# A Strassen step over pairs of FFN tiles in an RWKV layer: the products on block 11 of two tiles done as seven of 256 columns

## The chip, the cores and the metric

The kernel runs on one core of a Trainium2 chip. Its time is the device time of one execution in microseconds (us). The median of three runs of the kernel before is 3050.48 us (3047.41 to 3051.21). One further execution was taken with the hardware profiler, and all views of the trace below are of that one. The core's engines are TensorE (PE; its weight loads are listed as PEld), VectorE (DVE), ScalarE (ACT), GpSimd (POOL) and SyncE (SP, which here only issues DMAs). Each engine works through its instructions in order.

## The reference

A layer of 4 batches of 2048 tokens with 512 channels, all in float32: layer norm, then an RWKV attention and a feed-forward part (FFN) side by side, both added to the input.

```python
xn = _layernorm(x)
x = x + attn(xn) + ffn(xn)

def attn(x):
    r, k, v = (einsum('btc,hc->bth', mu * x + (1 - mu) * shifted, W) for ...)
    wkv = wkv_v4(k, v, w, u)        # a scan over the tokens
    return einsum('bth,ch->btc', sigmoid(r) * wkv, Wo)

def ffn(x):
    up_gate = einsum('bsd,hd->bsh', x, W1)   # 512 -> 2048
    up_lin = einsum('bsd,hd->bsh', x, W3)
    hidden = fwht(silu(up_gate) * up_lin)
    return einsum('bsh,dh->bsd', hidden, W2) # 2048 -> 512
```

## The kernel before, in words

The tokens are done in eight blocks of 1024 (`TB`), each in two halves of 512 (`H`). Channels lie on the 128 partitions. Blocks 0 and 1 also make and store combined weights; blocks 2 to 7 (the third and later ones) are alike. A block does, in this order:

- tile 0 of the gate and linear part, then six pairs of projections for k, v and r (`projected_pair`, line 410),
- tiles 1 to 15 of the gate and linear part (`up`, line 440): tile j gives 128 channels of `silu(gate) * linear` for both halves of the block, in the buffer `unit(j)` with its halves h0 and h1,
- the down part (`down`, line 727), which multiplies by W2 (with the Hadamard transform folded in) and Wo, in 46 pieces.

A gate and linear tile is one 2 x 2 block product, its left side the gate and linear weights of the tile, its right side the two halves of the tokens. It is done in Strassen-Winograd form: seven products in place of eight (`seven`, line 352), each over `KH` = 2 blocks of 128 channels and 512 columns, that is two matmuls. A matmul in float32 shows as two MATMUL rows in the trace, so a product is four rows. The weights of a tile come as one chunk of seven forms (896 KB) into a ring of three chunks (`ring_a`); `group` (line 971) asks for the chunk two ahead.

The seven products go into five PSUM banks, named pa, pf, pb, pc and pd. `bank()` (line 115) hands the eight banks out in turn. In the order of the code a tile does:

1. pa: form 0 on m11 (this is the product "on 11"); ACT copies pa to pb
2. pf: form 4; ACT copies pf to s5, in SBUF
3. pb: form 5; ACT copies pb to pc; then the **tail** of the tile before: ACT does the tanh of its pc into h1, DVE does one step on h0 with pd and two on h1 with pc and pb
4. pa: form 1; ACT does the tanh of pa into h0
5. pb: form 3; ACT copies pb to pd; DVE does `h0 = (h0 + 1) * pa`, then `step()`, then `pb += s5`
6. pc: form 6; DVE does `pc += s5`, then `step()`
7. pd: form 2

The recurrence of the attention runs on DVE (with exponentials on ACT) between these steps. `wkv(h)` (line 268) is a generator of nine pieces for each of the four heads of 128 channels; `step()` (line 968) issues the next one. The projections' hooks take nine pieces, the first head; the 15 tiles offer 30 places for the other 27. Since every engine works in order, the place of a `step()` in the code is its place on DVE's queue.

In the down part six of the seven forms are split once more ("deep", line 687), into matmuls of 256 columns, whose weights come in pieces into eight slots (`pieces_w`, `piece`, line 563). The first seven pieces are asked for at tile 15 (line 1053).

Of the kernel before, what the change touches and what calls it, by code (L numbers as in the profile page):

```python
# [2 lines left out]

# [6 lines left out]
F32 = mybir.dt.float32  # L10
# [5 lines left out]
P = 128  # L16
H = 512
# [23 lines left out]
def tile_rwkv_attn_hadamard_ffn(  # L41
# [36 lines left out]

    down_w = dram.tile([2, 7, KH, P, QR, P], F32, name="down_w")
    deep_w = dram.tile([6, 7, P, QR, P], F32, name="deep_w")  # L80
    stat_d = dram.tile([n_blocks, 2, TB], F32, name="stat_d")


# [6 lines left out]
    sa, sb = (const.tile([P, OFF + TB], F32, name=n) for n in ("sa", "sb"))  # L90
    e1b, e1 = (const.tile([P, TB], F32, name=n) for n in ("e1b", "e1"))
    banks = [ps.tile([P, H], F32, name=f"bank{b}") for b in range(8)]
    turn = [0]

    NP = NF // 2

    def unit(j):
        return right[:, j // NP, j % NP, :]
# [14 lines left out]
        return flat[:, 0:size].rearrange(f"p ({' '.join(names)}) -> p {' '.join(names)}", **dict(zip(names, shape)))  # L113

    def bank():
        turn[0] += 1
        return banks[(turn[0] - 1) % 8]


    k_flat, v_flat = (t.rearrange("p b t -> p (b t)") for t in (k_sb, v_sb))  # L120
    tf_flat = tf.rearrange("p f k t -> p (f k t)")
    x_first, x_tok = (flat.rearrange("p (t c) -> p t c", c=C) for flat in (k_flat, tf_flat))
    spread = v_sb[:, 0:2, :]
    stage = [v_sb[:, 2 + s // 2, ts(s % 2, H)] for s in range(4)]
    u2_of = [e1b[:, ts(g, H)] for g in range(KH)]
# [257 lines left out]
    def seven_forms(t, a11, a12, a22, a21):  # L383

        sub = ALU.subtract
        pool.tensor_tensor(t[1], a21, a22, ALU.add)
        pool.tensor_tensor(t[2], t[1], a11, sub)
        pool.tensor_tensor(t[3], a12, t[2], sub)
        pool.tensor_tensor(t[0], a11, a21, sub)
# [1 line left out]
    def forms_in(t):  # L391
        seven_forms([t[:, n] for n in range(3, 7)], *(t[:, n] for n in range(4)))

    def load_parts(i, n):
        t = ring_a.tile([P, 7, KH, P], F32, tag="a", name=f"part_{i}_{n}")
        if is_first(i, n):
            sp.dma_start(out=t[:, 0:4], in_=wpart[n])
            forms_in(t)
        else:
            sp.dma_start(out=t, in_=part_w[n])  # L400
        return t

    def is_first(i, n):
        return i == (1 if n < 3 * KH else 0)
# [35 lines left out]
    def up(i, j, w, tail, step):  # L440

        keep_parts(i, 3 * KH + j, w)
        h0, h1 = unit(j)[:, 0:H], unit(j)[:, H:TB]

        def on11(pa):
            act.activation(h0, pa, AF.Tanh, scale=0.5)

        def on22(pa, pb, s5):
            dve.scalar_tensor_tensor(h0, h0, 1.0, pa, ALU.add, ALU.mult)
            step()  # L450
            dve.tensor_tensor(pb, pb, s5, ALU.add)

        def on12(pc, s5):
            dve.tensor_tensor(pc, pc, s5, ALU.add)
            step()

        pb, pc, pd = seven(f"{i}_{j}", w, right_of["up"], tail, on11, on22, on12)
        return (
            lambda: act.activation(h1, pc, AF.Tanh, scale=0.5),
            lambda: dve.tensor_tensor(h0, h0, pd, ALU.mult),  # L460
            lambda: dve.scalar_tensor_tensor(h1, h1, 1.0, pc, ALU.add, ALU.mult),
            lambda: dve.tensor_tensor(h1, h1, pb, ALU.mult),
        )

# [93 lines left out]
        program += deep(m, *which)  # L560
    DEEP_AT = (0, 4, 5, 6, 1, 3, 2)

    def piece(i, u):

        return pieces_w[:, (u + 4 - len(program if i else whole_program)) % 8]

    def load_piece(i, u):
        pieces = program if i else whole_program
        if u < len(pieces):
            kind, form, n = pieces[u]  # L570
            src = down_w[n[0], form, n[1]] if kind == "plain" else deep_w[form, DEEP_AT[n]]
            sp.dma_start(out=piece(i, u), in_=src)

    whole, lo, hi = slice(0, H), slice(0, H // 2), slice(H // 2, H)
    x11, x12, x22 = stage[0:2], stage[2:4], x22_of
# [9 lines left out]
    def difference(out, x0, x1):  # L585
        dve.tensor_tensor(out, x0, x1, ALU.subtract)
# [8 lines left out]
    class Down:  # L595
# [21 lines left out]
            self.matmuls(pt, self.u - 1, rows, cols, start)  # L617

        def matmuls(self, pt, u, rows, cols, start=False):
            w = piece(self.i, u)  # L620
            for n in range(QR):
                pe.matmul(
                    pt[:, cols], lhsT=w[:, n, :], rhs=rows[:, n, :], start=start and n == 0, stop=n == QR - 1,
                    skip_group_check=True,
                )
# [299 lines left out]
    diag_1 = first_diagonals(1, first_statistics(1))  # L925

    def order_of(i):
        rkv, (first, *rest) = range(3 * KH), range(3 * KH, 3 * KH + NF)
        return [first, *rest] if i == 0 else [first, *rkv, *rest]

    class Chores:

# [26 lines left out]
    for i in range(n_blocks):  # L959
        last = i + 1 == n_blocks  # L960
        if i % per_batch == 0:
            dve.memset(carry[:, :, 0:1], PP0)
            dve.memset(carry[:, :, 1:3], 0.0)


        pieces = (None for h in range(NB) for _ in wkv(h))

        def step():
            next(pieces, None)

        def group(n):

            order = order_of(i)
            if n + 2 < len(order):
                parts.append(load_parts(i, order[n + 2]))
            return parts.pop(0)


        tail = ()
        if i == 0:  # L980
            for kind, after in ((1, 2), (2, 0), (0, None)):
                w = w_next
                if after is not None:
                    w_next = load_square(i, after)
                    if kind != 1:
                        mixed(after)
                if kind == 2:
                    for _ in token_forms(pool):
                        pass
                for n in range(2 * NB):  # L990
                    if kind == 1:
                        if n == NB - 1:
                            spread_1 = first_spread(diag_1)
                        if n == NB:
                            left = fold_products(3, 5)
                            first_normalized(1, spread_1)
                            fold_evict(left)
                            mixed(2)
                        projected(kind, w, n % NB, n // NB)
                    else:  # L1000
                        projected(kind, w, n // 2, n % 2)
                    if kind == 2 and n == 2:
                        fold_evict(fold_products(5, NP))
                        folded = fold_butterflies()
            parts = [load_parts(i, n) for n in order_of(i)[:2]]
        else:


            def mix_chores(*kinds):
                for kind in kinds:  # L1010
                    mix_before(kind, 0)
                    for b in range(NB):
                        if b + 1 < NB:
                            mix_before(kind, b + 1)
                        mix_here(kind, b)
                        yield
                    yield from mix_forms(kind)

            for b in range(NB):
                mix_here(1, b)  # L1020
            k_forms = mix_forms(1)
            tail = up(i, 0, group(0), tail, lambda: next(k_forms))
            for _ in k_forms:
                pass
            chores, hooks = mix_chores(2, 0), [0]
            for n in range(3 * KH):

                def hook():
                    hooks[0] += 1
                    for _ in range(1 if hooks[0] % 3 else 2):  # L1030
                        next(chores, None)
                    if hooks[0] in (5, 6, 8, 11, 12, 13, 14, 15, 17):
                        step()

                tail = projected_pair(i, n, group(1 + n), tail, hook)


        for j in range(0 if i == 0 else 1, NF):
            w = group(j if i == 0 else 3 * KH + j)
            if i == 0 and j <= NR:  # L1040
                if j > 1:
                    keep_down()
                if j < NR:
                    t = down_parts(0) if j == 0 else t_next
                    keep_down = down_forms(j, folded, t)
                    if j == 0:
                        keep_down()
                    t_next = down_parts(j + 1) if j + 1 < NR else None
            if i == 1 and j in (3, 5, 7, 9, 11, 13):
                keep_deep(j // 2 - 1, t)  # L1050
            if i == 1 and j in (1, 3, 5, 7, 9, 11):
                t = deep_forms(j // 2)
            if j == NF - 1:
                for u in range(7):
                    load_piece(i, u)
            tail = up(i, j, w, tail, step)
        for f in tail:
            f()
        for _ in pieces:
            pass  # L1060


        def next_parts():
            if not last:
                parts.extend(load_parts(i + 1, n) for n in order_of(i + 1)[:2])

        if not last:
            load_tokens(i + 1)
        if i == 0:
            down_whole(i, Chores(i + 1), next_parts)  # L1070
        else:
            down(i, Chores(i + 1), next_parts, last)
# [53 lines left out]
```

## Time and profile before

| what | value |
|---|---|
| median of three runs | 3050.48 us (3047.41 to 3051.21) |
| the profiled execution: time | 3048.46 us |
| the profiled execution: span, from the first to the last instruction | 3046.7 us |
| one block, third and later (tile 0 of the fourth block starts at 1176.05 us) | 372.6 us |
| tiles 1 to 15 of a block (15 tiles of 12.02 us) | 180.3 us |
| granted TensorE clock, mean | 0.999 |
| mean DMA rate over the span | 131 GB/s |

How to read the lines: in a timeline, the first two columns are the start and the time taken in us, then come the engine, the code line (all instructions have line 35, a helper's), the operation, what it writes and reads by the program's names, its shape, and how many such instructions the entry stands for; in square brackets stands how long the engine was idle before, and what released it. A matmul's end is modelled and lies after the start of the next one, since matmuls are pipelined: prices are therefore read from start to start. A table of windows gives for each stretch its length and then, for PE, PEld, DVE, ACT and POOL, the busy time and the number of instructions, then the granted clock, the DMA share and GB/s.

### The profile page before, as it was taken

What the parts mean: (1) busy time and instruction counts of PE and PEld (TensorE: products, weight loads), DVE (VectorE), ACT (ScalarE), POOL (GpSimd) and SP (SyncE); (2) the same over time, 40 slices, a digit from 0 to 9 for tenths busy, and PEclk for the clock granted to TensorE, in tenths of its full rate; (3) what the DMA queues carried; (4) which work ended last, traced back from release to release, by engine and by line L of the source; (5) the groups of instructions that cost most, each with busy time, mean ns of one, the idle gap of its engine ahead of it and who ended that gap; (6) DMA issues with size and microseconds to landing.
All of it is one profiled execution on the core that took longest, in us unless ns stands there. A gap on an engine that the chain in (4) does not pass through costs nothing.

```text
span 3046.7 us, 24404 instructions
## 1 busy us (share of the span) xinstructions
PE 3027.2 (99%) x8492; PEld 1613.7 (53%) x8492; DVE 2468.0 (81%) x2579; ACT 1014.6 (33%) x1822; POOL 231.9 (8%) x192
## 2 busy tenths in 40 slices
PE   8999999999999999999999999999999999999999
PEld 3444444447644476444854448544484445844458
DVE  6798658897888888888887978789798887988876
ACT  4233224333243323433233332433324333243321
POOL 3363003220000000000000000000000000000000
PEclk9999999999999999999999999999999999999999
DMA  4264524666422264222632236322453224522234
GB/s 174 74 204 170 189 82 136 215 215 216 137 75 82 79 233 132 73 77 101 224 120 80 73 133 201 110 80 78 161 166 117 73 81 165 184 93 78 73 123 143
DMA packets 136058, 397.64 MB, mean 131 GB/s; under 512 B 14336, under 2 KB 32768, under 8 KB 133760
## 3 DMA queue, kind: packets, MB, share of 16 engines
q1 hardware_dynamic: 135936, 396.09, 37.8%
q8 instruction: 68, 1.11, 0.1%
q14 instruction: 54, 0.44, 0.0%
HBM read 336.08 MB, written 59.96 MB: 130 GB/s over the span
## 4 chain that ended last, share of the span: by engine, by line
PE 95%; DVE 3%; DMA 1%; POOL 1%; ACT 0%; issue 0%; SPq 0%; POOLq 0%; ACTq 0%; DVEq 0%
PE bank L35 95%; DMA pieces_w<-deep_w 1%; DVE right L35 1%; DVE e1b L35 1%; POOL rs L35 1%; DVE e L35 0%; DVE xnT L35 0%; DMA stat_d<-rs 0%; DVE sb L35 0%; DVE sa L35 0%; DVE bank L35 0%; DVE v_sb L35 0%; DMA right<-w 0%; SPq L35 0%; ACT tf L35 0%
## 5 line engine op out<-in xcount | busy, mean ns | idle before, releaser
L35 PE MATMUL bank<-tf,part 128*128 128x512 f32 x2048 | 941.7, 592 | 0.0
L35 ACT COPY bank<-bank 128x512 f32<-128x512 f32 (+1 forms) x638 | 337.1, 528 | 1414.2 <-PE bank L35 1383.7
L35 PE MATMUL bank<-right,pieces_w 128*128 128x256 f32 (+1 forms) x2928 | 791.5, 430 | 3.1 <-DVE v_sb L35 2.5
L35 PE MATMUL bank<-xnT,part 128*128 128x512 f32 x1536 | 722.1, 592 | 1.1 <-DVE right L35 1.1
L35 PEld LDWEIGHTS bank<-right,pieces_w 128*128 128x128 f32 x2928 | 557.0, 190 | 230.9 <-issue 166.9
L35 PEld LDWEIGHTS bank<-tf,part 128*128 128x128 f32 x2048 | 389.0, 190 | 490.1 <-issue 461.8
L35 PEld LDWEIGHTS bank<-xnT,part 128*128 128x128 f32 x1536 | 291.6, 190 | 366.9 <-issue 358.2
L35 DVE TENSOR_TENSOR right<-right 128x1280 f32<-128x1280 f32 (+2 forms) x236 | 327.8, 1415 | 64.7 <-PE bank L35 63.7
L35 PE MATMUL bank<-right,part 128*128 128x512 f32 x840 | 369.6, 593 | 0.0
L35 DVE SCALAR_TENSOR_TENSOR right<-right,bank 128x512 f32<-128x512 f32 x256 | 174.4, 681 | 220.5 <-ACT right L35 220.3
L35 PEld LDWEIGHTS bank<-right,part 128*128 128x128 f32 x840 | 158.4, 190 | 203.2 <-issue 189.4
L35 ACT ACTIVATE right<-bank 128x512 f32<-128x512 f32 x308 | 183.8, 600 | 124.1 <-PE bank L35 105.7
L35 DVE RECIPROCAL e1b<-e1b 128x512 f32<-128x512 f32 x64 | 214.1, 3347 | 1.1
L35 DVE TENSOR_TENSOR bank<-bank,s 128x512 f32<-128x512 f32 x256 | 168.7, 690 | 37.4 <-ACT bank L35 23.8
L35 DVE TENSOR_TENSOR right<-right,bank 128x512 f32<-128x512 f32 x256 | 173.5, 678 | 11.5 <-PE bank L35 7.1
L35 POOL TENSOR_SCALAR mean<-sums 128x8 f32<-128x8 f32 x7 | 5.8, 835 | 1870.3 <-ACT tf L35 1518.6
L35 DVE SCALAR_TENSOR_TENSOR right<-xnT,vec,right 128x1024 f32<-128x1024 f32 x92 | 119.6, 1336 | 14.3 <-ACT right L35 14.3
L35 ACT COPY s<-bank 128x512 f32<-128x512 f32 x128 | 75.0, 586 | 144.9 <-PE bank L35 144.8
L35 POOL TENSOR_TENSOR part<-part 128x256 f32<-128x256 f32 x88 | 89.4, 1027 | 200.9 <-DMA part<-wpart 99.3
L35 ACT ACTIVATE right<-xnT,omm 128x1024 f32<-128x1024 f32 x92 | 100.3, 1143 | 12.3 <-PE bank L35 12.3
L35 PE MATMUL bank<-pieces_w,part 128*128 128x512 f32 x224 | 100.7, 592 | 0.0
L35 PE MATMUL bank<-k_sb,pieces_w 128*128 128x256 f32 x420 | 97.5, 379 | 0.0
(120 smaller groups left out, 2297.9 us busy)
## 6 DMA issues: line engine op xcount, KB each, us to landing
part<-part_w SPq DMA_DIRECT2D x148, 896.0 KB, 4.6
pieces_w<-deep_w SPq DMA_DIRECT2D x294, 320.0 KB, 3.2
pieces_w<-down_w SPq DMA_DIRECT2D x80, 320.0 KB, 5.4
part_w<-part SPq DMA_DIRECT2D x22, 896.0 KB, 6.0
tf<-x SPq DMA_DIRECT2D x7, 2048.0 KB, 7.8
xnT<-xT SPq DMA_DIRECT2D x7, 2048.0 KB, 10.0
deep_w<-pieces_w SPq DMA_DIRECT2D x6, 2240.0 KB, 10.3
v_sb<-xT SPq DMA_DIRECT2D x48, 256.0 KB, 8.0
```

Source lines behind the costliest of these rows:

```text
L35: return self.tc.keep_in_program_order(issue(*args, **kwargs))
```

## The change

Blocks 2 to 7 do tile 0 as before, tile 1 as a single one, and tiles 2 to 15 as seven pairs. Two tiles of a pair share the right side of the product on 11, so their two products, four matmuls of 512 columns, are one 2 x 2 block product again (its rows the two tiles, its inner index the two blocks of 128 channels, its columns the two halves of the 512). It is done in seven matmuls of 256 columns (`Pair.step`), into two banks, one for each tile (`rows`); they are spread over the tiles ahead. Block 0 makes the four extra weight forms of each pair (`make_pair`, on POOL) and stores them in DRAM (`pair_w`). A pair then loads three chunks, of one 448 KB and twice 768 KB; all of them go through the ring of three. The banks come from a list, first in, first out: `take()` takes one, `give()` puts it back at the end. In the new tile (`up_rest`) the first `step()` stands behind the tail, before the products on forms 1 and 3.

```diff
-    turn = [0]
+    free_banks = deque(banks)
...
     def bank():
-        turn[0] += 1
-        return banks[(turn[0] - 1) % 8]
+        free_banks.rotate(-1)
+        return free_banks[-1]
+
+    def take():
+        return free_banks.popleft()
+
+    def give(*pts):
+        free_banks.extend(pts)
...
+    def make_pair(p, w0, w1):
+        (a11, a12), (a21, a22) = ([w[:, 0, b] for b in range(KH)] for w in (w0, w1))
+        seven_forms([pair_forms[:, n] for n in range(4)], a11, a12, a22, a21)
+        sp.dma_start(out=pair_w[p - 1][:, 0:2], in_=w0[:, 0])
+        sp.dma_start(out=pair_w[p - 1][:, 2], in_=w1[:, 0, 1])
+
+    def keep_pair(p):
+        sp.dma_start(out=pair_w[p - 1][:, 3:7], in_=pair_forms)
...
+    def up_rest(which, tail, step):
...
+        yield
+        if pa is None:
+            pa = take()
+            product(pa, 0, m11, True)
+            for f in tail:
+                f()
+            tail = ()
+        pb = take()
+        act.copy(pb, pa)
+        pf = take()
+        product(pf, 4, f1, True)
+        s5 = small.tile([P, H], F32, tag="s5", name=f"s5_{key}")
+        act.copy(s5, pf)
+        give(pf)
+        yield
+        product(pb, 5, f2)
+        pc = take()
+        act.copy(pc, pb)
+        for f in tail:
+            f()
+        step()
+        yield
+        product(pa, 1, m21)
+        act.activation(h0, pa, AF.Tanh, scale=0.5)
+        yield
+        product(pb, 3, f3)
+        dve.scalar_tensor_tensor(h0, h0, 1.0, pa, ALU.add, ALU.mult)
+        give(pa)
+        pd = take()
+        act.copy(pd, pb)
+        dve.tensor_tensor(pb, pb, s5, ALU.add)
+        yield
+        product(pc, 6, m22)
+        dve.tensor_tensor(pc, pc, s5, ALU.add)
+        step()
+        yield
+        product(pd, 2, f4)
+        return (
+            lambda: act.activation(h1, pc, AF.Tanh, scale=0.5),
+            lambda: dve.tensor_tensor(h0, h0, pd, ALU.mult),
+            lambda: dve.scalar_tensor_tensor(h1, h1, 1.0, pc, ALU.add, ALU.mult),
+            lambda: dve.tensor_tensor(h1, h1, pb, ALU.mult),
+            lambda: give(pd, pc, pb),
+        )
+
+    def pair_quarters():
+        return [b11[:, b, cols] for b in range(KH) for cols in (lo, hi)]
+
+    def make_pair_sums():
+        q11, q12, q21, q22 = pair_quarters()
+        t1, t2, t3, t4 = (pair_sums[:, n] for n in range(4))
+        for out, x, y in ((t1, q12, q11), (t2, q22, t1), (t3, q22, q12), (t4, q21, t2)):
+            difference(out, x, y)
+
+    class Pair:
...
+        def step(self, *which):
...
+            for n in which:
+                if n == 1:
+                    self.rows = [take(), take()]
+                a, b = self.rows
+                pt, right = (
+                    (a[:, lo], q11), (a[:, hi], t1), (b[:, hi], t2), (a[:, hi], q22), (a[:, lo], q21), (b[:, hi], t3), (b[:, lo], t4),
+                )[n]
+                pe.matmul(pt, lhsT=self.w[:, DEEP_AT[n]], rhs=right, start=n == 1, stop=True, skip_group_check=True)
+                if n == 0:
+                    act.copy(b[:, hi], a[:, lo])
+                elif n == 1:
+                    act.copy(pair_s5, a[:, hi])
+                elif n == 2:
+                    act.copy(a[:, hi], b[:, hi])
+                elif n == 5:
+                    act.copy(b[:, lo], b[:, hi])
+                elif n in (3, 6):
+                    dve.tensor_tensor((a, b)[n == 6][:, hi], (a, b)[n == 6][:, hi], pair_s5, ALU.add)
+
+    def up_pairs(i, chunk, tail, step):
+
+
+        def run(which, woven):
+            rest = up_rest(which, tail, step)
+            for n in range(6):
+                next(rest)
+                for f in woven.get(n, ()):
+                    f()
...
+        which = single(1)
+        chunk.load(1)
+        tail = run(which, {1: [lambda: begin(1)], 2: [deep(0)], 3: [deep(2)], 4: [deep(5, 4, 3)]})
+        for p in range(1, n_pairs):
+            pair, more = pairs[-1], p + 1 < n_pairs
+            which = tile(pair, 0)
+            chunk.load(1)
+            woven = {0: [lambda: pair.step(6), lambda: chunk.load(1)]}
+            if not more:
+                woven[0].append(lambda: [load_piece(i, u) for u in range(7)])
+            else:
+                woven[5] = [lambda: begin(p + 1)]
+            tail = run(which, woven)
+            which = tile(pair, 1)
+            if more:
+                chunk.load(1)
+            tail = run(which, {0: [deep(0)], 2: [deep(2)], 4: [deep(5, 4, 3)]} if more else {})
+        return tail
...
-    def piece(i, u):
-
-        return pieces_w[:, (u + 4 - len(program if i else whole_program)) % 8]
+    def piece(u):
+        return pieces_w[:, u % 8]
...
+        if i >= 2:
+            make_pair_sums()
+            tail = up_pairs(i, chunk, tail, step)
+        for j in range(i, NF) if i < 2 else ():
+            if i == 0 and j % 2 and j > 1:
+                keep_pair(j // 2)
+            if i == 0 and j % 2 == 0 and j > 0:
+                make_pair(j // 2, *parts.values())
+            w = group(("full", 3 * KH + j))
```

`begin(p)` makes the Pair with its chunk and does `step(1)`; `deep(...)` does the named steps of the newest pair. Of a pair's chunks, the two "rest" ones leave form 0 out.

More of the change, by code (lines that the diff above doesn't have):

```diff
@@ L1 @@
+from collections import deque
 from contextlib import ExitStack
@@ L80, in tile_rwkv_attn_hadamard_ffn @@
     deep_w = dram.tile([6, 7, P, QR, P], F32, name="deep_w")
+    pair_w = dram.tile([NF // 2 - 1, P, 7, P], F32, name="pair_w")
     stat_d = dram.tile([n_blocks, 2, TB], F32, name="stat_d")
@@ L122, in tile_rwkv_attn_hadamard_ffn @@
     x_first, x_tok = (flat.rearrange("p (t c) -> p t c", c=C) for flat in (k_flat, tf_flat))
+    pieces_flat = pieces_w.rearrange("p u q c -> p (u q c)")
+    pair_sums = pieces_flat[:, 0 : 2 * H].rearrange("p (n t) -> p n t", n=4)
+    pair_s5 = pieces_flat[:, ds(7 * QR * P, H // 2)]
+    pair_forms = pieces_flat[:, ds(7 * KH * P, 4 * P)].rearrange("p (f c) -> p f c", f=4)
     spread = v_sb[:, 0:2, :]
@@ L392, in forms_in, with load_parts @@
         seven_forms([t[:, n] for n in range(3, 7)], *(t[:, n] for n in range(4)))
-    def load_parts(i, n):
-        t = ring_a.tile([P, 7, KH, P], F32, tag="a", name=f"part_{i}_{n}")
-        if is_first(i, n):
+    def load_parts(i, chunk):
+        kind, n = chunk
+        t = ring_a.tile([P, 7, KH, P], F32, tag="a", name=f"part_{i}_{kind}_{n}")
+        if kind == "pair":
+            sp.dma_start(out=t.rearrange("p f k c -> p (f k) c")[:, 0:7], in_=pair_w[n - 1])
+        elif kind == "rest":
+            sp.dma_start(out=t[:, 0:6], in_=part_w[n][:, 1:7])
+        elif is_first(i, n):
             sp.dma_start(out=t[:, 0:4], in_=wpart[n])
@@ L463, in up, with product @@
         )
+    def up_rest(which, tail, step):
+        key, j, lhs, pa = which
+        m11, m21, m22, f1, f2, f3, f4 = right_of["up"]
+        h0, h1 = unit(j)[:, 0:H], unit(j)[:, H:TB]
+        def product(pt, form, right, start=False):
+            for b in range(KH):
+                pe.matmul(
+                    pt, lhsT=lhs(form)[:, b, :], rhs=right[:, b, :], start=start and b == 0, stop=b == KH - 1,
+                    skip_group_check=True,
+                )
[42 more added lines that the diff above has]
+            lambda: give(pd, pc, pb),
+        )
@@ new lines, in pair_quarters, with __init__ @@
+    def pair_quarters():
[6 more added lines that the diff above has]
+    class Pair:
+        def __init__(self, i, p, w):
+            self.i, self.p, self.w = i, p, w.rearrange("p f k c -> p (f k) c")
+        def step(self, *which):
+            q11, _, q21, q22 = pair_quarters()
+            t1, t2, t3, t4 = (pair_sums[:, n] for n in range(4))
+            for n in which:
[16 more added lines that the diff above has]
+                    dve.tensor_tensor((a, b)[n == 6][:, hi], (a, b)[n == 6][:, hi], pair_s5, ALU.add)
@@ new lines, in up_pairs, with single, tile, deep @@
+    def up_pairs(i, chunk, tail, step):
[5 more added lines that the diff above has]
+                    f()
+            try:
+                next(rest)
+            except StopIteration as end:
+                return end.value
+        def single(j):
+            w = chunk(("full", 3 * KH + j))
+            return f"{i}_{j}", j, lambda form: w[:, form], None
+        def tile(pair, row):
+            j = 2 * pair.p + row
+            w = chunk(("rest", 3 * KH + j))
+            return f"{i}_{j}", j, lambda form: w[:, form - 1], pair.rows[row]
+        n_pairs = NF // 2
+        def deep(*ns):
+            return lambda: pairs[-1].step(*ns)
+        pairs = []
+        def begin(p):
+            pairs.append(Pair(i, p, chunk(("pair", p))))
+            pairs[-1].step(1)
+        which = single(1)
[16 more added lines that the diff above has]
+        return tail
@@ L571, in load_piece @@
             src = down_w[n[0], form, n[1]] if kind == "plain" else deep_w[form, DEEP_AT[n]]
-            sp.dma_start(out=piece(i, u), in_=src)
+            sp.dma_start(out=piece(u), in_=src)
     whole, lo, hi = slice(0, H), slice(0, H // 2), slice(H // 2, H)
@@ L619, in matmuls @@
         def matmuls(self, pt, u, rows, cols, start=False):
-            w = piece(self.i, u)
+            w = piece(u)
             for n in range(QR):
@@ L927, in order_of @@
     def order_of(i):
-        rkv, (first, *rest) = range(3 * KH), range(3 * KH, 3 * KH + NF)
-        return [first, *rest] if i == 0 else [first, *rkv, *rest]
+        first, *rest = (("full", 3 * KH + j) for j in range(NF))
+        rkv = [("full", n) for n in range(3 * KH)]
+        if i < 2:
+            return [first, *rest] if i == 0 else [first, *rkv, *rest]
+        pairs = [(kind, n) for p in range(1, NF // 2) for kind, n in (("pair", p), *(("rest", 3 * KH + 2 * p + k) for k in range(2)))]
+        return [first, *rkv, rest[0], *pairs]
     class Chores:
@@ L969, in step, with load_more, chunk, group @@
             next(pieces, None)
[L971 to L976, printed above, removed]
+        order = order_of(i)
+        def load_more(n):
+            for _ in range(min(n, len(order) - loaded[0])):
+                parts[order[loaded[0]]] = load_parts(i, order[loaded[0]])
+                loaded[0] += 1
+        def chunk(which):
+            taken[0] += 1
+            return parts.pop(which)
+        chunk.load, taken = load_more, [0]
+        def group(which):
+            load_more(taken[0] + 3 - loaded[0])
+            return chunk(which)
         tail = ()
@@ L1004, in tile_rwkv_attn_hadamard_ffn @@
                         folded = fold_butterflies()
-            parts = [load_parts(i, n) for n in order_of(i)[:2]]
+            parts = {n: load_parts(i, n) for n in order_of(i)[:2]}
+            loaded = [2]
         else:
@@ L1021, in tile_rwkv_attn_hadamard_ffn @@
             k_forms = mix_forms(1)
-            tail = up(i, 0, group(0), tail, lambda: next(k_forms))
+            tail = up(i, 0, group(("full", 3 * KH)), tail, lambda: next(k_forms))
             for _ in k_forms:
@@ L1033, in hook @@
                         step()
-                tail = projected_pair(i, n, group(1 + n), tail, hook)
-        for j in range(0 if i == 0 else 1, NF):
-            w = group(j if i == 0 else 3 * KH + j)
+                tail = projected_pair(i, n, group(("full", n)), tail, hook)
+        if i >= 2:
[7 more added lines that the diff above has]
+            w = group(("full", 3 * KH + j))
             if i == 0 and j <= NR:
@@ L1064, in next_parts @@
             if not last:
-                parts.extend(load_parts(i + 1, n) for n in order_of(i + 1)[:2])
+                parts.update((n, load_parts(i + 1, n)) for n in order_of(i + 1)[:2])
+                loaded[0] = 2
         if not last:
```

## The prediction

> **What bounds the kernel now.** First the page's head: TensorE (PE) is busy for the whole span, at a granted clock of 0.999.
>
> ```profile
> span 3046.7 us, 24404 instructions
> PE 3027.2 (99%) x8492; PEld 1613.7 (53%) x8492; DVE 2468.0 (81%) x2579; ACT 1014.6 (33%) x1822; POOL 231.9 (8%) x192
> ```
>
> Blocks from the third on repeat every 372.6 us, and the change touches their gate and linear tiles. So second the busy times of one such stage (fourth block, tiles 1 to 15 from 1260.3 us; columns: window, then PE, PEld, DVE, ACT busy):
>
> ```profile
> 1284.00:1308.00 24.00, 24.00 (x58) 10.61 (x57) 16.55 (x20) 8.74 (x14) 0.00 (x0) 1.00 0.23 77
> 1308.00:1332.00 24.00, 24.00 (x58) 10.61 (x57) 23.76 (x23) 8.70 (x14) 0.00 (x0) 1.00 0.23 77
> ```
>
> PE is never idle, but DVE (VectorE) goes from two thirds to 99% within a tile or two: the recurrence's pieces come in lumps. Less PE work is therefore less time only while DVE stays ahead of what PE waits for.
>
> Third, TensorE's timeline gives the prices (start, time, what, rows):
>
> ```profile
> 1132.88 13.11 PE L35 MATMUL bank<-right,pieces_w 128*128 128x256 f32 x60
> 1145.83 2.32 PE L35 MATMUL bank<-tf,pieces_w 128*128 128x256 f32 x10
> ...
> 1296.37 1.88 PE L35 MATMUL bank<-xnT,part 128*128 128x512 f32 x4
> 1298.09 3.60 PE L35 MATMUL bank<-tf,part 128*128 128x512 f32 x8
> 1301.52 1.88 PE L35 MATMUL bank<-xnT,part 128*128 128x512 f32 x4
> ```
>
> From start to next start, 8 rows of 512 columns take 3.43 us, 0.429 each; 60 rows of 256 take 12.95, 0.216 each. A matmul in the code is two rows. Call a product of a tile (two matmuls of 512, four rows) u = 1.717 us, and one matmul of 256 columns d = 0.432 us. A tile of seven products is 12.02 us.
>
> **What goes.** A pair of tiles loses two products on 11 (2u = 3.43 us) and gains seven small matmuls (7d = 3.02): 0.41 us less, times 7 pairs and 6 blocks: **-17.2 us**. Half the columns cost half the time here. The Trainium skill speaks against it: "TensorE: Matmul & The Clock Gate", section "Back-to-back issue gap", has a sustained 81 ns at 128 columns and 131 ns at 512; on a line between them 256 columns cost 0.75 of 512, the pair would lose 1.05 us and the change 44 us; 0.216 beside 0.429 in this trace contradicts that, and I go by the rows.
>
> **What is added off PE.** Per pair four ACT copies of 256 columns (0.36 each) and two DVE sums (0.42); per block four DVE differences for the right sides (0.42 each). ACT is at a third, and DVE's sum, 148 us in the 181 of the stage, rises by 7.6: both fit on average. Loads grow by 0.2 MB a pair, at 77 GB/s now. A pair's chunk is asked for when its ring slot comes free, 0.4 us into an even tile, and needed 9.0 us into it; part loads land in 3.3 to 8.9 us, median 4.6: hidden, by 4 us at the median, at worst 0.3 us late. In the first block POOL gets four 128-column operations a pair (below the 1.03 us of 256 columns, so at most 4.1 a 24 us pair) and SP three issues (0.33 to 0.45 each); POOL's fullest 20 us there hold 17.4, and parts are made two tiles ahead: nothing (if the cover fails, at most 4 us a pair for a few pairs). Pieces' slots turn by two and their seven loads come one tile sooner, when nothing else stands on SP till the next block's loads: nothing.
>
> **What is late next: a bank.** Before, the eight PSUM banks go round, five a tile, and a bank has most of a tile to be read. Now a pair holds two banks across tiles. I followed the free list, first in, first out: at the start of every odd tile of a pair it holds two, the pb of the odd tile before and the **pa of the even tile just done**; pb of the new tile takes the first, **pf the second**. PE's second action in an odd tile, the product into pf, thus waits for the last reader of pa, the DVE step on h0; all of PE's work is queued behind it. And that step now stands behind a recurrence piece, since step() moved from after it to before it. Its normal place and what runs before it (fifth tile; ACT, then DVE):
>
> ```profile
> 1301.72 0.57 ACT L35 COPY bank<-bank 128x512 f32<-128x512 f32 x1 [1.13 <-PE bank L35]
> 1302.21 0.60 ACT L35 ACTIVATE right<-bank 128x512 f32<-128x512 f32 x1
> ```
> ```profile
> 1302.84 0.69 DVE L35 SCALAR_TENSOR_TENSOR right<-right,bank 128x512 f32<-128x512 f32 x1 [2.92 <-ACT right L35]
> 1303.57 0.69 DVE L35 TENSOR_TENSOR right<-right,bank 128x512 f32<-128x512 f32 x1
> 1304.17 0.68 DVE L35 SCALAR_TENSOR_TENSOR right<-right,bank 128x512 f32<-128x512 f32 x1
> 1304.77 1.22 DVE L35 TENSOR_TENSOR e1b<-e,sb 128x1024 f32<-128x1024 f32 x1
> 1306.02 1.23 DVE L35 TENSOR_TENSOR e1b<-e1b,k_sb 128x1024 f32<-128x1024 f32 x1
> 1307.28 3.35 DVE L35 RECIPROCAL e1b<-e1b 128x512 f32<-128x512 f32 x1
> 1310.55 1.27 DVE L35 TENSOR_TENSOR bank<-bank,s 128x512 f32<-128x512 f32 x2
> ```
>
> The product on form 5 ends at 1301.52; ACT copies, then does the earlier tile's tanh; DVE's tail starts 1.32 us after that end, takes 1.33, then h0 (0.68, third line), then the piece. A new even tile is 6u + 2d = 11.17 us, an odd one 6u + 5d = 12.46. In the even tile form 5 ends at d + 2u = 3.87, the tail runs 5.19 to 6.52, then the piece P, then h0: done at 7.20 + P, PE going on 0.14 later (below). PE wants pf at 11.17 + d = 11.60. **It waits if P is over 4.26 us, or if DVE is late already.**
>
> Pieces by start to next start: 1 (first scan) 3.7, 2 5.0, 3 and 5 none (exponentials on ACT), 4 3.8, 6 3.7, 7 5.8, 8 3.3, 9 4.9. The nine projection hooks use up head 0; then two a tile, first of a tile (A) and second (B): tile 4 A7 B8, 5 A9 B1, 6 A2 B3, 7 A4 B5, 8 A6 B7, 9 A8 B9, 10 A1 B2, 11 A3 B4.
> - Tile 4: 7.20 + 5.78 + 0.14 = 13.12 against 11.60: tile 5 waits **1.5**.
> - Tile 6, DVE counted from tile 4's start: h0 starts at 12.30; h0 and two steps on PSUM (0.60 to the next start, each) 14.1; piece 8 17.35; tail's first step 17.95; tail's rest 19.3; piece 9 24.2; h0, step, sum (0.4), step 26.4; piece 1 30.1; sum 30.5; tail's first 31.1, its rest 32.4; piece 2 37.45; h0 done 38.13, and 0.14. Tile 6 starts 13.12 + 12.03 = 25.15 and PE wants pf 11.60 later, at 36.75: tile 7 waits **1.5**.
> - Tile 8: 7.20 + 3.65 = 10.85, no wait, but pieces 7, 8, 9, 1 follow. Tile 10, from tile 8's start in the same way: h0 and two steps to 11.97, piece 7 17.75, tail 19.7, piece 8 22.9, h0 to the last step 25.1, piece 9 30.0, sum and tail 32.4, piece 1 36.1, h0 done 36.75, and 0.14; PE wants pf at 11.17 + 12.46 + 11.60 = 35.23: tile 11 waits **1.7**.
> - Tiles 2 and 12 have an exponential at A; tile 14 begins no pair, so its pa is not next.
> - Tile 1: the four differences come after the projections' last DVE step (starts 1263.21, 0.60 to the next); the first is done at 1264.23, PE wants it after two products, 1260.32 + 3.43 = 1263.75, and 0.14 more: **0.6**.
>
> Sum 5.3 us a block, against 2.87 saved: +2.4, times 6 = **+14.6 us**. That PE does wait so is in the trace: in the second block, where POOL slows DVE (first scan 3.45 for 2.35), the reuse of a bank stops it (DVE, then PE):
>
> ```profile
> 584.93 0.69 DVE L35 TENSOR_TENSOR right<-right,bank 128x512 f32<-128x512 f32 x1
> ```
> ```profile
> 583.50 1.88 PE L35 MATMUL bank<-tf,part 128*128 128x512 f32 x4
> 585.67 1.98 PE L35 MATMUL bank<-xnT,part 128*128 128x512 f32 x4 [0.30 <-DVE right L35]
> 587.49 3.81 PE L35 MATMUL bank<-tf,part 128*128 128x512 f32 x8
> ```
>
> PE, due at 585.22, starts 0.05 after DVE's end and needs 1.82 instead of 1.72 for the product: 0.14 in all. Bounds of what the trace lacks: a wait of this form could cost nothing beyond DVE's lateness (0.1 less each), or 0.3 more each, as the second product's stretch from 3.43 to 3.65 shows when ACT is late too: 4 x 6 x 0.1 = -2.4 to +7 us; the DVE sum on PSUM (0.42 taken; 0.34 to 0.69) moves a wait by 0.3 at most.
>
> **Rivals.** *Only the saving* (0.10): if DVE's h0 always beats PE's pf, the time is 3048.5 - 17.2 = 3031. It decides from waits under 2.87 us a block on, and under 1.9 it is faster by what can be measured; for it, DVE has 33 us of 181 free; against it, piece 7 alone is 5.78 long and stands straight before h0. *A draw* (0.15): the waits come to 2 to 3.9 us, if DVE's order frees pa a microsecond sooner in each: about 3048. *More waits* (0.13): pair chunks land late, or ACT's copies, queued behind exponentials, hold PE: one more microsecond in every second tile is 7 a block less what DVE gains by it, some 3 x 6 = 18 more: 3080. That the small matmuls don't cost half is in the last one's end.
>
> **The numbers.** The forecast has 0.62. The profiled run took 3048.46 us, span plus 1.8: plus 14.6 it is 3063; the median shown is 2.0 above that run, so I say 3064, between the two bases. Measurement tells 0.2%, 6.1 us, from no change. Slower: 0.62 + 0.13 = 0.75; within: 0.15; faster: 0.10. Range 3046 to 3075: from inside the draw to the bounds of the waits above.
>
> **What would show it.** PE's busy share in the stage falls below 100%, with four waits a block on DVE, in tiles 1, 5, 7 and 11, of 0.6 to 1.7 us, the last three at the first 512-column product after one of 256 columns; tile pairs without them last 23.6 us; 256-column rows stay at 0.216. It is wrong if tiles 5, 7 and 11 start their second product without a gap, or if gaps stand at other places.

## The result

The kernel with the change takes 3066.22 us (median of four runs, 3065.20 to 3068.25) beside 3050.16 for the kernel before: a ratio of 1.0057, interval 1.0044 to 1.0069, 16.1 us slower. The forecast was 3064 us, its range 3046 to 3075.

The page of the kernel after, its head:

```profile
span 3066.5 us, 25293 instructions
PE 3018.7 (98%) x8744; PEld 1659.8 (54%) x8744; DVE 2514.0 (82%) x2687; ACT 1060.5 (35%) x1990; POOL 253.1 (8%) x220
```

TensorE (PE) has 8.5 us less work by its busy time and yet ends 19.8 us later in the profiled execution (3068.25 us, the slowest of the four): so work was saved, and idle time came that was not there (busy time also counts rows that run longer behind a wait, so it isn't the price of the matmuls; E6 below has that). The chain of waits, by engine and line, says with whom PE waits:

```profile
PE 83%; DVE 15%; ACT 1%; DMA 1%; issue 0%; POOL 0%; SPq 0%; ACTq 0%; DVEq 0%
```

A share of 15% for DVE (3% before) doesn't mean that PE stood still for that long; it means that the work that ended last goes back through stretches of DVE's queue. Where PE stood still is in its timeline (same block as in the prediction; tile 1 starts at 1268.39 here):

```profile
1270.10 1.88 PE L36 MATMUL bank<-tf,part_full 128*128 128x512 f32 x4
1272.35 0.70 PE L36 MATMUL bank<-pieces_w,part_pair 128*128 128x256 f32 x2 [0.36 <-DVE pieces_w L36]
1273.16 1.98 PE L36 MATMUL bank<-tf,part_full 128*128 128x512 f32 x4
...
1318.79 0.59 PE L36 MATMUL bank<-xnT,part_pair 128*128 128x256 f32 x2
1320.60 3.70 PE L36 MATMUL bank<-tf,part_rest 128*128 128x512 f32 x8 [1.22 <-DVE right L36]
...
1343.90 0.60 PE L36 MATMUL bank<-xnT,part_pair 128*128 128x256 f32 x2
1345.61 3.70 PE L36 MATMUL bank<-tf,part_rest 128*128 128x512 f32 x8 [1.11 <-DVE right L36]
...
1392.52 0.60 PE L36 MATMUL bank<-xnT,part_pair 128*128 128x256 f32 x2
1394.39 3.70 PE L36 MATMUL bank<-tf,part_rest 128*128 128x512 f32 x8 [1.27 <-DVE right L36]
```

The four places are tiles 1, 5, 7 and 11. The number in brackets is idle time after the modelled end of the matmul before, so the loss is read from starts: a matmul of 256 columns takes 0.43 to the next start, so 1318.79 should be followed by 1319.22 and is by 1320.60; and the two products after it take 3.54 in place of 3.43. That makes 1.49 us in tile 5, 1.38 in tile 7, 1.54 in tile 11. In tile 1 it is 0.53 before the small matmul, 0.38 after it and 0.10 more, 1.01. With 0.07 in tile 14 a block loses 5.5 us; tiles 1 to 15 take 182.84 us for 180.25, 2.6 more a block, 15.6 in six.

DVE in the even tile ahead of the wait in tile 5 (its order is tail, piece 7, h0):

```profile
1312.81 0.69 DVE L36 SCALAR_TENSOR_TENSOR right<-right,bank 128x512 f32<-128x512 f32 x1 [1.31 <-ACT right L36]
1313.53 0.69 DVE L36 TENSOR_TENSOR right<-right,bank 128x512 f32<-128x512 f32 x1
1314.14 1.22 DVE L36 TENSOR_TENSOR e1b<-e,sb 128x1024 f32<-128x1024 f32 x1
...
1316.65 3.35 DVE L36 RECIPROCAL e1b<-e1b 128x512 f32<-128x512 f32 x1
1319.92 0.63 DVE L36 SCALAR_TENSOR_TENSOR right<-right,bank 128x512 f32<-128x512 f32 x1
```

The last line is the step on h0, the last reader of pa. It ends at 1320.55, PE's product into that bank starts at 1320.60.

What is left of the profiled execution's 19.8 lies mostly in the second block, whose gate and linear tiles the change leaves as they were. PE is idle there for 4.13 us before 638.17, and its clock is halved behind that, which costs 2.7 us more (last section). The kernel before had idle times of 0.3 to 0.5 us in tiles near there. While POOL makes deep weights, DVE's steps of 1.22 us take 2.44, and on which steps that falls differs: PE is idle in the same place for 1.8, 1.35 and 0.5 us in the profiles of E1, E6 and E12 below. The three other runs of the change are 2 to 3 us shorter.

### The profile page after: what moved, and what is told of

The parts are those of the page before. It is cut to its first block, busy times and chain, and to the rows that moved or that the text cites. A ratio compares the mean times of both kernels' runs of the same rounds, so it can differ in the third digit from the quotient of the medians.

```text
span 3066.5 us, 25293 instructions
## 1 busy us (share of the span) xinstructions
PE 3018.7 (98%) x8744; PEld 1659.8 (54%) x8744; DVE 2514.0 (82%) x2687; ACT 1060.5 (35%) x1990; POOL 253.1 (8%) x220
## 4 chain that ended last, share of the span: by engine, by line
PE 83%; DVE 15%; ACT 1%; DMA 1%; issue 0%; POOL 0%; SPq 0%; ACTq 0%; DVEq 0%
PE bank L36 83%; DVE right L36 5%; DVE e1b L36 4%; DVE e L36 2%; DVE bank L36 1%; DVE sb L36 1%; DVE sa L36 1%; ACT bank L36 0%; DMA pieces_w<-deep_w 0%; DVE v_sb L36 0%; ACT right L36 0%; DVE k_sb L36 0%; DVE xnT L36 0%; POOL rs L36 0%; DMA right<-w 0%
## 5 line engine op out<-in xcount | busy, mean ns | idle before, releaser
L36 PE MATMUL bank<-tf,part_rest 128*128 128x512 f32 x1344 | 619.2, 594 | 21.6 <-DVE right L36 21.6
L36 PEld LDWEIGHTS bank<-tf,part_rest 128*128 128x128 f32 x1344 | 253.6, 190 | 301.3 <-issue 239.5
L36 PE MATMUL bank<-right,part_full 128*128 128x512 f32 x840 | 369.6, 594 | 0.0
L36 PE MATMUL bank<-tf,part_full 128*128 128x512 f32 x704 | 326.3, 595 | 0.7
L36 PE MATMUL bank<-xnT,part_rest 128*128 128x512 f32 x672 | 315.8, 592 | 0.0
L36 PEld LDWEIGHTS bank<-right,part_full 128*128 128x128 f32 x840 | 158.6, 190 | 203.0 <-issue 189.3
L36 PE MATMUL bank<-xnT,part_full 128*128 128x512 f32 x528 | 250.0, 596 | 4.1 <-DVE right L36 4.1
L36 PEld LDWEIGHTS bank<-tf,part_full 128*128 128x128 f32 x704 | 133.8, 191 | 167.3 <-issue 155.0
L36 PEld LDWEIGHTS bank<-xnT,part_rest 128*128 128x128 f32 x672 | 127.8, 190 | 129.9 <-issue 126.2
L36 PEld LDWEIGHTS bank<-xnT,part_full 128*128 128x128 f32 x528 | 100.8, 191 | 123.5 <-issue 115.5
```

Of the source, the lines that this page charges most:

```text
L36: return self.tc.keep_in_program_order(issue(*args, **kwargs))
```

## The experiments

All are beside runs of the kernel before on the same chip (medians 3048.72 to 3050.16). Gaps are those of the third block, from starts as above; in E2 and E7 they hold 1.7 us each of a halved clock (last section).

| run | us | ratio to before (interval) | gaps a block, us |
|---|---|---|---|
| the change | 3066.22 | 1.0057 (1.0044 to 1.0069) | 5.5 |
| E1 step back | 3045.68 | 0.9986 (0.9977 to 0.9995) | 2.2 |
| E2 early sums | 3083.39 | 1.0105 (1.0091 to 1.0119) | 8.7 |
| E3 swap | 3051.67 | 1.0006 (0.9997 to 1.0015) | 3.2 |
| E4 before, step moved | 3048.14 | 0.9996 (0.9988 to 1.0005) | 0 |
| E5 before, quiet | 3050.16 | 1.0003 (0.9994 to 1.0012) | 0 |
| E6 change, quiet | 3033.10 | 0.9948 (0.9935 to 0.9961) | 0 |
| E7 E1 + E2 | 3063.44 | 1.0052 (1.0039 to 1.0065) | 5.3 |
| E8 E2 + step split | 3058.12 | 1.0030 (1.0019 to 1.0042) | 3.3 |
| E9 late tail | 3066.35 | 1.0058 (1.0045 to 1.0070) | 5.7 |
| E10 E2 + E9 | 3063.47 | 1.0044 (1.0031 to 1.0056) | 5.1 |
| E11 E8 + E9 | 3041.80 | 0.9971 (0.9962 to 0.9980) | 1.4 |
| E12 E11 + second step | 3037.03 | 0.9958 (0.9946 to 0.9971) | 0.6 |

The theory is that PE waits because the bank it wants is freed by a DVE step that stands behind a recurrence piece. Its rival is that DVE simply has too much to do, wherever the pieces stand.

**E1, the first step() back behind the step on h0.**

```diff
         for f in tail:
             f()
-        step()
...
         give(pa)
+        step()
         pd = take()
```

> The first step() of a tile goes back behind DVE's step on h0, banks as in the change. Bank theory (PE waits because pa, the bank that pf needs, is freed by a DVE step behind a recurrence piece): the waits in tiles 5, 7 and 11 (1.5, 1.4, 1.5 us) go; tile 1 keeps 0.9; the sum on the next pair's bank now comes later in odd tiles, which costs some 0.75 in tile 6 and 0.4 in tile 14. 2.1 us a block against 2.87 saved: about 5 us faster than before, 3045. Load theory (DVE has too much to do wherever the pieces stand): the waits move to other tiles with the same sum, about 3066.

3045.68. The waits in tiles 5, 7 and 11 are gone, and those that were worked out for the sums are there: 0.70 in tile 6 and 0.39 in tile 14 (0.75 and 0.4 expected). In the timeline of the third block, tile 6's (PE's releaser is ACT's copy of pa to pb, which itself had waited for the sum on pa until 955.32):

```profile
953.66 1.88 PE L36 MATMUL bank<-tf,part_rest 128*128 128x512 f32 x4
955.98 1.98 PE L36 MATMUL bank<-tf,part_rest 128*128 128x512 f32 x4 [0.44 <-ACT bank L36]
```

DVE does the same work in this kernel as in the change, and PE gets 20.5 us back. The rival falls.

**E2, the four differences ahead of the projections' last piece.**

```diff
                 def hook():
                     hooks[0] += 1
+                    if i >= 2 and hooks[0] == 17:
+                        make_pair_sums()
...
         if i >= 2:
-            make_pair_sums()
             tail = up_pairs(i, chunk, tail, step)
```

> The four differences for the pairs' right sides are put before the projections' last recurrence piece, the rest as in the change. Bank theory: tile 1's wait of 0.9 us goes, tiles 5, 7 and 11 keep theirs: 6 x 0.9 = 5.5 us less than the change, about 3061. Load theory: the same DVE work, so the time stays at 3066.

3083.39: wrong by 22 us, and the wrong way. The small matmul in tile 1 no longer waits, but the product after it does, longer. E8 has the same start; there ACT and then PE in tile 1 of the third block:

```profile
893.75 0.63 ACT L36 ACTIVATE right<-right 128x512 f32<-128x512 f32 x1 [3.75 <-DVE right L36]
894.28 0.58 ACT L36 COPY bank<-bank 128x512 f32<-128x512 f32 x1
```
```profile
892.11 0.59 PE L36 MATMUL bank<-pieces_w,part_pair 128*128 128x256 f32 x2
894.92 1.98 PE L36 MATMUL bank<-tf,part_full 128*128 128x512 f32 x4 [2.21 <-ACT bank L36]
```

The activation at 893.75 is the tanh of d12, one quarter of the last projection's result. In tile 1, and only there, `up_rest` issues the tail ahead of the copy of pa to pb. So ACT waits 3.75 us for DVE with the copy behind it, and PE waits for the copy. The four differences, moved ahead of the last piece, made DVE 1.5 us later with d12. That longer wait (2.47 us a block for 1.01) is half of the 17 us that E2 takes over the change; the other half is PE's clock, halved behind it in five of the six blocks (last section). In the change itself the same chain ends tile 1's gap. Its chain of waits (start, time, what) has DVE's last two steps ahead of the differences, the second of them on d12, then d12's tanh, ACT's copy and PE:

```profile
1270.13 1.83 DVE right L36 x2
1271.99 0.63 ACT right L36
1272.62 0.49 ACT bank L36
1273.16 38.51 PE bank L36 x102
```

**E3, two take() calls swapped in odd tiles.**

```diff
-        pb = take()
-        act.copy(pb, pa)
-        pf = take()
+        if j % 2 and j > 1:
+            pf, pb = take(), take()
+        else:
+            pb, pf = take(), take()
+        act.copy(pb, pa)
```

> Only the order of two take() calls in a pair's odd tile: pf gets the bank that is long free, pb the one of pa, which is wanted 1.7 us later but needs 0.7 us of ACT's copy first. DVE's queue is untouched. Bank theory: the waits in tiles 5 and 11 shrink by 1.0 us each; tile 7's stays near 1.5, since DVE works without a break from tile 4 to 6, so that PE, a microsecond earlier, waits a microsecond more. 6 x 2.0 = 12 us less than the change, about 3054. Load theory: no difference, 3066.

3051.67, 14.6 us less than the change (12 expected). Tiles 5 and 11 wait 0.37 and 0.41 instead of 1.5. Tiles 6 and 7 wait 0.30 and 1.01, together 1.31, near the 1.5 expected of tile 7: in a stretch where DVE never rests, PE's being earlier only moves its wait. No instruction of DVE changed place or size here; which bank is handed out decides 14.6 us.

**E4, the kernel before with the step moved.**

```diff
+        early = i >= 2 and j > 0
+        if early:
+            tail = (*tail, step)
         pb, pc, pd = seven(f"{i}_{j}", w, right_of["up"], tail, on11, on22, on12)
```

with `step()` in `on22` only `if not early`.

> The kernel before, with only the first step() of tiles 1 to 15 of blocks 2 to 7 moved behind the tail, as the change has it; its eight banks go round as before. Bank theory: pa's bank is wanted again 9 us after that, so the order alone costs nothing: 3050. If the order of DVE's queue by itself is what costs: up to 4.5 us a block, about 3065 to 3077.

3048.14, no difference, no gap. So the order of DVE's queue costs nothing by itself (E4), the banks held by pairs cost little by themselves (E1), and the two together cost 20 us.

**E5 and E6, both kernels without the pieces.**

```diff
         def step():
-            next(pieces, None)
+            if i < 2:
+                next(pieces, None)
...
-        for _ in pieces:
+        for _ in pieces if i < 2 else ():
             pass
```

> The kernel before, with the recurrence's pieces of blocks 2 to 7 left out (the attention's recurrence isn't computed there). Both theories: PE was never idle in these stages, so the time stays at 3050.

> The change, with the same pieces left out (the recurrence isn't computed in blocks 2 to 7). What the matmuls alone are worth: if a matmul of 256 columns costs half of one of 512 among them too, 17.2 us less than the quiet kernel before, about 3033, and no gaps in tiles 1 to 15. If small matmuls between large ones cost more, or the pair's ACT copies hold PE, a part of it is missing.

3050.16 and 3033.10: the pairs' matmuls are worth 17.1 us, the forecast's term was 17.2. With DVE at rest, PE has no gap in tiles 1 to 15.

**E7, E1 and E2 together.** 

> The change with both: first step() behind the step on h0, and the four differences early. Bank theory: only the sums' waits in tiles 6 and 14 are left, 1.2 us a block against 2.87 saved: 10 us faster than before, 3040. Load theory: 3066.

3063.44, wrong by what E2 was wrong by, 17.8 us over E1.

**E8, E2 and the first step() split:** behind h0 in even tiles, behind the pair's sum in odd ones.

```diff
         for f in tail:
             f()
-        step()
...
         give(pa)
+        if j % 2 == 0:
+            step()
...
-            tail = run(which, {0: [deep(0)], 2: [deep(2)], 4: [deep(5, 4, 3)]} if more else {})
+            tail = run(which, {0: [deep(0)], 2: [deep(2)], 4: [deep(5, 4, 3), step]} if more else {4: [step]})
```

(and the same in tile 1.)

> The change with the differences early and the first step() placed by what PE needs next: in even tiles behind the step on h0, which frees pa, in odd tiles (and tile 1) behind the pair's sum. Bank theory: no DVE step that PE waits for stands behind a piece any more; nearly all of the 17.2 us comes out, 3033 to 3036. Load theory: 3066; DVE does the same work in all of these.

3058.12, over 20 us more than expected. Tiles 5, 6, 11 and 14 have no gap. Tile 1 has E2's 2.5, and a new one of 0.8 stands in tile 7 (ACT, then PE, third block):

```profile
963.50 1.06 ACT L36 ACTIVATE e1b<-e1b 128x1024 f32<-128x1024 f32 x1 [1.40 <-DVE e1b L36]
964.46 0.35 ACT L36 COPY pieces_w<-bank 128x256 f32<-128x256 f32 x1
```
```profile
962.45 1.88 PE L36 MATMUL bank<-tf,part_rest 128*128 128x512 f32 x4
964.87 0.70 PE L36 MATMUL bank<-xnT,part_pair 128*128 128x256 f32 x2 [0.54 <-ACT pieces_w L36]
```

The copy to the pair's s5 stands behind an exponential that waits for DVE, and the next small matmul, into the other half of the bank, waits for the copy. 3.3 us a block make 3052.8; the rest is a clock that halved after the long wait (last section).

**E9, E10, the projections' tail late.**

```diff
             product(pa, 0, m11, True)
-            for f in tail:
-                f()
-            tail = ()
```

> The change, with one thing else: in tile 1 the projections' tail stands behind the copy of pb to pc, as in all other tiles, not ahead of the copy of pa to pb. New theory of tile 1: its second gap, and the 2.4 us that the early differences cost, come from ACT: the tail holds a tanh of the last projection's d12, which waits for DVE, and the copy to pb stands behind it. Then the small matmul's wait for the differences (0.5) stays, what follows it (0.4) goes: 2 us less than the change, 3064. If the pair's differences alone make tile 1's gap: no difference, 3066.

> The change with the differences early and the projections' tail late, step() as in the change. New theory of tile 1: no gap in tile 1 at all, the three bank waits stay: 6 x 1.0 less than the change, 3060. If the early differences are what costs 17 us, through DVE: 3083 as before.

3066.35 and 3063.47; neither came out as written. The gap behind the first small matmul is gone in both, as is E2's 2.4 us: E10 is 19.9 us under E2 with one edit. But ACT's three steps of the tail now stand ahead of the copy from bank a to b, and the third small matmul of tile 1 waits 0.6 for that. So E9 gains nothing (1.23 for 1.01 in tile 1), and E10 keeps 0.6 of 1.01. Where the tail stands decides which product it holds up.

**E11, E8 with the tail late.** 

> Differences early, projections' tail late, first step() behind the step on h0 in even tiles and behind the pair's sum in odd ones. Left over is one wait of 0.8 us a block in tile 7, where the first small matmul waits for ACT's copy to the pair's s5, which stands behind exponentials that wait for DVE: 3050 - 17.2 + 4.8 = 3038.

3041.80; the 0.8 of tile 7 was expected, tile 1's 0.6 not: 1.4 a block, 3050 - 17.2 + 8.4 = 3041.2.

**E12, the second step() of even tiles in the next tile,** behind ACT's copies:

```diff
         dve.tensor_tensor(pc, pc, s5, ALU.add)
-        step()
+        if j % 2:
+            step()
...
-            ... {0: [deep(0)], 2: [deep(2)], ...
+            ... {0: [deep(0)], 1: [step], 2: [deep(2)], ...
```

> As the one before, and the second step() of an even tile goes behind the first large product of the next tile, so that the exponentials come after ACT's copies that PE waits for; DVE's queue is the same. Bank theory with the two of ACT: no gap in tiles 1 to 15, 3033, as the quiet kernel. Load theory: not under 3050.

3037.03, ratio 0.9958 (0.9946 to 0.9971): faster than the kernel before, by 13 us, and than the change, by 29. DVE has as many instructions as in the change (2687). The busy times of 180 us of this stage, in the fourth block (columns as in the prediction's windows):

```profile
1262.00:1442.00 180.00, 179.66 (x468) 88.59 (x467) 155.85 (x181) 72.77 (x136) 0.00 (x0) 1.00 0.27 94
```

In the change, its 182.8 us from 1268.4 have PE at 178.72 and DVE at 154.12. The place where tile 5 waited in the change now reads, in the third block:

```profile
938.23 0.59 PE L36 MATMUL bank<-xnT,part_pair 128*128 128x256 f32 x2
938.66 3.60 PE L36 MATMUL bank<-tf,part_rest 128*128 128x512 f32 x8
```

0.43 from start to start, no wait. What is left is tile 1's 0.6, which makes 3.6 us in six blocks; the expectation, with no gap at all, was 4 us too low.

## Why the prediction was right

- **The saving**, 17.2 us: E6 against E5 shows 17.1. Rows of 256 columns cost 0.216 to the next start among rows of 512 too. The figures that the prediction quoted from the Trainium skill ("TensorE: Matmul & The Clock Gate", "Back-to-back issue gap"), with its straight line between them, would have made it a loss; the runs contradict that.
- **The bank**, three waits of 1.5, 1.5 and 1.7 us: 1.49, 1.38 and 1.54, in the tiles named and on the step named. E3 and E1 confirm the two halves of the cause, the bank that is handed out and the piece ahead of h0; E4 shows that the second alone is harmless.
- **Tile 1**, 0.6 us: 1.01. Here the size was off and the cause half wrong. The differences do hold the small matmul for 0.5 us, as worked out. The other half is ACT: the prediction didn't follow ACT's queue in tile 1, where the projections' tail stands ahead of the copy to pb. E2, E9 and E10 showed it. The expectations of E2, E7 and E8, which left that queue out too, were 22 to 25 us too low.
- **What was costed at nothing** (the pairs' loads, the ACT copies, the first block's extra forms): E6 and E12 have them all, and E6 shows no gap in tiles 1 to 15. The profile of the change has no wait on a DMA in these stages. ACT's copies for the pairs are free only while nothing that waits stands ahead of them: 0.8 us a block in E8 and 0.6 in E12 are waits for such a copy.
- **The sum**, +14.6 by the profiled execution's own time: the medians differ by 16.1, and the six blocks' tiles alone give 15.6 in the profiles. That it came so near is in part luck: the three bank waits are 4.4 us a block for 4.7, tile 1 is 0.4 longer, and the two errors nearly cancel. The second block's longer wait was no term of the sum; it differs from run to run.
- The rivals: the saving alone is what E6 shows with the pieces left out; more waits, by exponentials ahead of ACT's copies, did not decide in the change, but did in E8, once PE no longer waited for the banks.

## What to carry to other kernels

When a change moves buffers from a round with slack to a list with none, follow the list by hand: which buffer is handed out next, which instruction reads it last, and what stands ahead of that instruction on its engine. An engine that is 82% busy is no limit until the one step that another engine waits for stands behind a lump of other work; placing the lump behind that step was worth 20 us here (E1), and with the like for ACT's queue 29 (E12), and took no work away. And each such mending moves the limit to the next queue, so that ACT has to be followed as DVE was.

## What the runs showed of the hardware

- **A short gap can halve PE's clock.** After tile 1's wait of 2.4 us in E8 (2.21 of it idle by the modelled ends), three of six blocks went on at half the rate (four rows of 512 columns in up to 3.2 us from start to start, for 1.72), and lost 1.7 us more; the other three went on at once. With it E8 adds up: 3046.7 - 17.2 + 6 x 3.3 + 3 x 1.7 = 3054.4, its span is 3054.3. In E2 and E7 it was five of six; in E10, E11 and E12, which don't have that wait, none.

  Which blocks they are can be read from the clock in the 14 profiles. Without the first 30 and the last 15 us of each, the granted clock falls to half 15 times, and within a trace the falls lie whole multiples of 3.413 us apart. Cut into stretches of that length, each stretch that ends in such a fall has at least 1.98 us without PE work; each other one entered at full clock has at most 1.95. So it matters how much of a wait lies within one stretch. Two blocks of E8, the waits' ends at 1267.96 and 1643.24, each with the stretch of the wait and the next (first the busy time of PE, then of PEld, DVE, ACT and POOL; the number after POOL's is the granted clock):

```profile
1265.98:1269.39 3.41, 1.43 (x4) 0.71 (x5) 0.78 (x2) 1.90 (x4) 0.00 (x0) 1.00 0.00 0
1269.39:1272.81 3.42, 3.42 (x7) 1.70 (x6) 0.00 (x0) 0.93 (x2) 0.00 (x0) 0.50 0.00 0
1641.45:1644.86 3.41, 1.62 (x4) 0.87 (x5) 0.59 (x1) 1.90 (x4) 0.00 (x0) 1.00 0.00 0
1644.86:1648.27 3.41, 3.41 (x11) 1.90 (x10) 0.23 (x1) 1.70 (x4) 0.00 (x0) 1.00 0.00 0
```

  PE is idle for 1.98 us of the first stretch and for 1.79 of the third. No run moved a wait against these stretches on purpose. The change's own waits in the pairs' tiles, up to 1.4 us, were never followed by a fall; its 4.13 us in the second block were. The Trainium skill ("TensorE: Matmul & The Clock Gate", "HAM oscillation — how this bites in real kernels") warns of idle gaps above some 3.4 us; here 2.2 us were enough in 13 of 18 cases.
- **PE resumes at once after a wait**: 0.05 us after DVE's end, and 0.10 to 0.11 lost over the next product.
